# Order of the first products of each pass, of the sums of their weights, and of cf's column sums

## The chip, the cores and the metric

One NeuronCore of one Trainium2 chip runs the whole program, in float32. The metric is the device time of one execution in microseconds (us); the kernel before takes 1213.07 us (median of three runs, 1211.28 to 1214.89). Engines: TensorE (PE, with its weight loads PEld), VectorE (DVE), ScalarE (ACT), GpSimd (POOL) and SyncE (SP, whose queue issues most transfers).

## The reference

x holds 32 sequences of 64 tokens with 1024 features. The layer is an attention block and an expert ffn, each behind a linear map with a low-rank addition:

```python
x = x + attn(cond(x, label))       # cond: x W1' + rank 32, by the sequence's label
x = x + ffn(cond2(x, language))    # cond2: x W2' + 8 experts of rank 16, top 2 by logits
# attn: q, k, v = x Wqkv' + b; rotary q, k; 32 heads of 32, 8 of k and v; causal softmax; Wo
# ffn:  x W3' + b + 8 experts of rank 16, top 2 by softmax
```

## The kernel before

**Folded weights.** A first stage, *gen*, multiplies consecutive linear maps together, so that the tokens pass each composed matrix once. Its multiplications are *cq* and *ckv* (W1 with Wqkv: 1024 × 1024 and 1024 × 512) and *cf* (W2 with W3, 1024 × 1024; the residual's identity is added on its diagonal). The composed matrices go to scratch memory in DRAM (cqkv, and cf7, which already holds the sums that the ffn's products need).

**Products.** Every large multiplication is a `Group` (line 231), which computes a 2 × 2 block product with seven block products instead of eight. A block product (`mult`, line 259) is four calls of matmul over the chunks of the inner dimension. In the profile that is eight MATMUL instructions, 3.43 us for 512 columns. The left factors are blocks of the weights ("11", "12", "22") or their sums s1 to s4, which `weight_sums` (line 172) makes on GpSimd with four instructions, in the order s1, s3, s2, s4 of lines 179, 181, 180, 182. The right factors are blocks of the tokens or of the other matrix, or their column sums t1 to t4, which `column_sums` (line 185) makes on VectorE, four instructions each, on lines 191, 193, 195, 197. The products accumulate in three PSUM banks x, y and z:

| step | product | bank | what follows |
|---|---|---|---|
| p1 | 11 × 11 | x | ScalarE copies it to a sum p (line 282) |
| p6 | s2 × t2 | y | VectorE: u1 = y + p (line 288) |
| p5 | s1 × t1 | z | |
| p7 | s3 × t3 | y | VectorE: u2 = y + p (line 300) |
| p2 | 12 × 21 | x | output (0,0) |
| p4 | 22 × t4 | y | output (1,0) |
| p3 | s4 × 22 | z, after output (1,1) has left it | output (0,1) |

**Two passes.** After gen, the loop over `hf` (line 897) takes 1024 tokens a pass. A pass begins with the 16 instructions of the column sums of x (line 912), and then the query and key projections in five pairs of 128-row blocks, first pair 4 (the keys), then pairs 0 and 1. `qk_pair(g)` (line 950) loads the pair's weights from cqkv (SyncE's queue), has their sums made on GpSimd and gives a `RankGroup` (line 375). Its `main(begun, held)` runs the steps p1, p6, p5, p7, p2, then the rank rows and the outputs (`together`), p4 and p3, from step number `begun` on. The output of each pair is rotated on VectorE and GpSimd (`rope`, line 930). In the first pass the weights of pairs 4 and 0 are loaded ahead, during gen. In the second pass, low-rank matmuls (`ranks`, line 448) are woven between p1, p6 and the rest. Weight tiles have two buffers, and so have their sums. Pairs 2 and 3, the attention units, v and the output projection follow.

**The ffn** ends a pass: seven block products, each cut into two quarters, each quarter again a Group. In a `quarter` (line 1385) the function `known` adds on GpSimd what is already known of an output to the sum just made (line 1407); VectorE adds that to the PSUM bank on line 1425, which frees the bank for the next product.

**What sets the order.** A planner orders each engine's instructions by program order, by when it reckons their inputs ready, and by a cost table. Inside `manual_schedule` the named engines keep the program's order: SyncE, TensorE and VectorE in gen; TensorE and GpSimd in the ffn; all engines from pair 2 to the end of the output projection. The first pairs of a pass lie between, and there the planner decides, except for TensorE's first steps in the second pass. `tc.issue_after(ins)` makes what its block issues on the engine of `ins` stand behind `ins` in that engine's queue. It orders the queue alone; instructions on other engines, transfers among them, are untouched.

Of the kernel before, what the change touches and what calls it, by code (L numbers as in the profile page):

```python
# [13 lines left out]
F32 = mybir.dt.float32  # L14
# [5 lines left out]
P = 128  # L20
# [56 lines left out]
def block_kernel(ctx: ExitStack, tc: tile.TileContext, a, out: bass.AP):  # L77
    nc = tc.nc
# [16 lines left out]
    def tmp(name):  # L95
        return tp.tile([P, 512], F32, tag="t", name=name)
# [5 lines left out]
    late = {}  # L102
# [12 lines left out]
    def load_x(hf):  # L115
        t = [xp.tile([P, TH], F32, tag=f"x{kc}", name=f"x{kc}_{hf}") for kc in range(KC)]
        for kc in range(KC):
            nc.sync.dma_start(t[kc], a["xT"][kc, :, hf * TH : (hf + 1) * TH])
        return t
# [6 lines left out]
            engines={mybir.EngineType.SP, mybir.EngineType.PE, mybir.EngineType.DVE}  # L126
# [104 lines left out]
    class Group:  # L231
# [26 lines left out]

        def mult(self, ps, left, right, first=False):
            for kc in range(self.h):  # L260
                nc.tensor.matmul(  # L261
                    ps,
                    self.weights[left][:, kc, :],
                    self.right(right, kc),
                    start=first and kc == 0,
                    stop=kc == self.h - 1,
                    skip_group_check=True,
                )
# [154 lines left out]
    def load_w(from_, name):  # L423
        w = wp.tile([P, KC, WG], F32, tag="w", name=f"w_{name}")
        nc.sync.dma_start(w, from_)
        return w
# [74 lines left out]
    def differences(dst, src, n):  # L501

        v = src[:, : n * 2 * P].rearrange("p (g r o) -> p g r o", r=2, o=P)
        nc.gpsimd.tensor_sub(dst, v[:, :, 0, :], v[:, :, 1, :])

    with tc.tile_pool(name="gen", bufs=1) as gen:
# [43 lines left out]
        def sums_of(name, right, n):  # L550

            t = Columns(halves(right, n), n // 2, H, [None] * 4)

            def make(*which):
                for j in which:
                    s = gen.tile([P, H, 512], F32, tag=f"sum{j}", name=f"sum{j}_{name}")
                    t.tiles[j] = [s[:, kc, :] for kc in range(H)]
                    for kc in range(H):
                        t.make(kc, (j,))

            return t, make
# [67 lines left out]
        t_cf, make_cf = sums_of("cf", w3, D)  # L629
# [54 lines left out]
        def load_w3(w):  # L684
# [6 lines left out]
                (0, "p1"): lambda w: b1kv_rows[1](),  # L691
                (0, "p7"): lambda w: done_later(),
                (1, "p4"): load_w3,
                (3, "out11"): lambda w: make_cf(0, 1),
            },
        )
        make_cf(2, 3)
        differences(b1d, b1q, 5)
        b2 = hp.tile([P, TH], F32, tag="hw", name="b2").rearrange("p (k o) -> p k o", o=P)
        nc.sync.dma_start(b2, a["b2"])  # L700
# [190 lines left out]
    def scoped(name, bufs=1, side="left"):  # L891
        return pools.enter_context(tc.tile_pool(name=name, bufs=bufs, side=side, reuse_waits="tile"))
# [4 lines left out]
    for hf in range(2):  # L897
        x = first_pass["x"] if hf == 0 else load_x(hf)
# [23 lines left out]
        def low_half(c, low=low):  # L922
            return low.rearrange("p (b c t) -> p b c t", c=2, t=S)[:, :, c, :]
# [26 lines left out]
        def qk_pair(g, z_bank=group_bank):  # L950
            w = first_pass.pop(f"w{g}", None)
            if w is None:
                w = load_w(cqkv[:, :, g * WG : (g + 1) * WG], f"qk{hf}{g}")

            def out(r, c, ps, add):
                oc = 2 * g + r
                raw = tmp(f"raw_{hf}_{oc}_{c}")
                bias = bqk[:, oc : oc + 1]
                if add is None:
                    nc.scalar.activation(raw, ps, AF.Identity, bias=bias)  # L960
                else:
                    nc.vector.scalar_tensor_tensor(raw, ps, bias, add, ALU.add, ALU.add)
                rope(oc, c, raw)

            def rank(r, c, rows):
                b = b1d[rows, g, :] if (r, c) == (0, 1) else b1q[rows, (2 * g + r) * P : (2 * g + r + 1) * P]
                return b, low_half(c)[rows]

            return RankGroup(f"qk{hf}{g}", w, weight_sums(w, f"qk{hf}{g}"), xt, out, rank, z_bank)
# [119 lines left out]
                    av[b].rearrange("p (i m t) -> p i m t", i=2, t=S),  # L1089
                )  # L1090

        pair = qk_pair(4)
        if hf == 0:
            pair.p1()
        else:
            with tc.manual_schedule(engines={mybir.EngineType.PE}):
                for do in first_halves:
                    do()
                pair.p1()
                for do in second_halves + (pair.p6,) + sums:  # L1100
                    do()
        pair.main(1 + hf)
        for g in (0, 1):
            held, pair = pair, qk_pair(g, (ps_tile, group_bank)[g])
            pair.main(held=held)
        pair.last_rows()
        pair.out01()
        if hf == 0:
# [62 lines left out]
        with tc.manual_schedule():  # L1171

            rotated()
            pair, held = qk_pair(2), None
            for u in range(2):
# [14 lines left out]
                if u == 0:  # L1190
                    held, pair = g, qk_pair(3, ps_tile)
# [14 lines left out]
            for u in range(4):  # L1206
                first, second = 2 * u + 1, 2 * u + 2
# [62 lines left out]
            yp = scoped(f"sums_y{hf}", side="right")  # L1270
# [87 lines left out]
        w = wp.tile([P, KC, WG], F32, tag="w", name=f"w_h{hf}")  # L1358
# [20 lines left out]
        hw, acc, ring = {}, {}, []  # L1379

        def accumulator(x):
            pool, tag = {"a": (yp, "sum3"), "b": (fp, "b"), "z": (yp, "sum2"), "c": (None, None)}[x]
            acc[x] = acc["a"] if x == "c" else pool.tile([P, 4, 512], F32, tag=tag, name=f"{x}_f{hf}")

        def quarter(n, q):

            step, _, _ = SEVEN[n]

            if len(ring) < 2:
                ring.append(wp.tile([P, KC, WG], F32, tag="w", name=f"w_f{hf}{q}"))  # L1390
            w = ring[q].rearrange("p s (k o) -> p s k o", o=P)
            for part in (slice(0, 3), slice(4, 8)):
                nc.sync.dma_start(
                    w[:, part].rearrange("p s k o -> p (s k) o"),
                    cf7[:, n, part, :, q].rearrange("p s k o -> p (s k) o"),
                )
            prior, kept = acc.get(PRIOR.get(step)), acc.get(KEPT.get(step))
            r, c = OUT.get(step, (None, None))
            outs = {}

            def part(t, m, half):
                return t[:, 2 * q + m, half * 256 : (half + 1) * 256]

            def known(m, half, add):
                if prior is not None:
                    to = part(prior if kept is None else kept, m, half)
                    nc.gpsimd.tensor_add(to, part(prior, m, half), add)

            def out_f(m, half, ps, add):
                if prior is not None:  # L1410
                    add = part(prior if kept is None or add is None else kept, m, half)
                if kept is not None:
                    if add is None:
                        nc.scalar.copy(part(kept, m, half), ps)
                    else:
                        nc.vector.tensor_add(part(kept, m, half), ps, add)
                    return
                oc = 4 * r + q + 2 * m
                both = m in outs
                if not outs and q:  # L1420
                    outs["pair"] = fp.tile([P, 2, 512], F32, tag="gates", name=f"o_{hf}_{step}")
                if not both:
                    outs[m] = outs["pair"][:, m] if q else tmp(f"o_{hf}_{oc}_{c}")
                o = outs[m][:, half * 256 : (half + 1) * 256]
                nc.vector.scalar_tensor_tensor(o, ps, bb[:, oc : oc + 1], add, ALU.add, ALU.add)
                if both:
                    nc.scalar.dma_start(out[oc, :, hf, c, :], outs[m])

            def extra(m, half):
                differs = (m, half) == (0, 1)  # L1430
                for i, b in enumerate(experts_b):
                    if step == "p3":
                        lhs = bd[:, i, 8 + q if differs else q + 2 * m]
                    elif differs:
                        lhs = bd[:, i, 4 + 2 * r + q]
                    else:
                        oc = 4 * r + q + 2 * m
                        lhs = b[:, oc * P : (oc + 1) * P]
                    yield lhs, hw[i][c][:, half * 256 : (half + 1) * 256]

            group = Quarter(
                f"f{hf}{n}{q}",
                {name: w[:, i] for i, name in enumerate(FACTORS)},
                None, ts[n], out_f, extra if step in OUT else None, known, (group_bank, ps_tile)[q],
            )
            group.n_q = n, q
            return group
# [15 lines left out]
        with tc.manual_schedule(engines={mybir.EngineType.PE, mybir.EngineType.Pool}):  # L1463
# [17 lines left out]
            for n in range(7):  # L1481
                step = SEVEN[n][0]
                if step in KEPT:
                    accumulator(KEPT[step])
# [125 lines left out]
```

## Time and profile before

| | before |
|---|---|
| median of three runs | 1213.07 us |
| the profiled execution | 1214.05 us |
| its span, first to last instruction | 1212.3 us |
| PE busy | 1191.3 us (98%) |
| DVE busy | 701.6 us (58%) |
| POOL busy | 533.7 us (44%) |
| mean granted TensorE clock | 0.996 |
| TensorE's waits for other engines, in total | 16.3 us |

All times inside the profile count from the start of the span. Gen reaches to about 298 us, the first pass to about 752 us, the second to the end. A group of instructions is written as output <- inputs by the program's names: `qk_x`, `qk_y`, `qk_z` are the banks of a query and key pair, `f_x` to `f_z` those of the ffn, `cf_x` to `cf_z` those of cf; `s_qk` are sums of weights, `sum_x` and `sum_cf` column sums, `w_qk` weights. Buffer numbers are left out, so pairs 4 and 0 have the same names. A wait names the engine and line that ended it.

### The profile page before, as it was taken

How to read it: one execution, taken by the hardware profiler on the slowest of the kernel's cores; microseconds unless marked ns; L12 is line 12 of the kernel's file. 1: busy time of each engine (PE TensorE's matmuls, PEld its weight loads, DVE VectorE, ACT ScalarE, POOL GpSimd, SP SyncE). 2: the span in 40 equal slices, each digit the busy share in tenths (PEclk: the TensorE clock that was granted, in tenths of full speed). 3: DMA queues.
4: the chain of work that ended last, by engine and by line, in shares of the span. 5: the costliest groups of instructions: out<-in, count | busy, mean ns of one | idle time of the engine just before them, and what ended most of it. 6: DMA issues, size and time to landing. Idle time of an engine off the chain costs nothing.

```text
span 1212.3 us, 15157 instructions
## 1 busy us (share of the span) xinstructions
PE 1191.3 (98%) x5916; PEld 705.9 (58%) x5916; DVE 701.6 (58%) x1221; ACT 156.6 (13%) x302; POOL 533.7 (44%) x477
## 2 busy tenths in 40 slices
PE   9999999999899999999999998999999999999998
PEld 3444864554344458644458887444458644448887
DVE  4312162619356788774657552556788864657562
ACT  1000000000000114530011000100113530011000
POOL 3341364242244655761814533434655761812231
PEclk9999999999899999999999999999999999999999
DMA  6662744858111120222316665121120222304543
GB/s 243 220 210 102 267 143 144 293 164 285 48 63 35 35 71 1 71 70 70 103 31 193 194 193 159 48 66 35 35 70 2 71 70 70 102 24 112 157 140 103
DMA packets 114679, 136.71 MB, mean 113 GB/s; under 512 B 6576, under 2 KB 92976, under 8 KB 113328
## 3 DMA queue, kind: packets, MB, share of 16 engines
q1 hardware_dynamic: 101120, 111.52, 28.9%
q10 hardware_dynamic: 10800, 15.84, 3.7%
q0 software_dynamic: 2688, 8.39, 2.1%
q8 instruction: 47, 0.77, 0.3%
q14 instruction: 24, 0.20, 0.0%
HBM read 101.02 MB, written 34.71 MB: 112 GB/s over the span
## 4 chain that ended last, share of the span: by engine, by line
PE 92%; DVE 4%; DMA 2%; issue 1%; POOL 0%; SPq 0%; DVEq 0%; POOLq 0%
PE qk_y L261 9%; PE o_y L261 7%; PE f_y L261 6%; PE qk_z L261 6%; PE qk_x L261 6%; PE v L990 5%; PE o_x L261 5%; PE o_z L261 5%; PE f_z L261 4%; PE f_x L261 4%; PE cq_y L261 3%; PE cf_y L261 3%; PE sc L1011 3%; PE pt L1064 2%; PE cq_z L261 2%; PE f_z L273 2%
## 5 line engine op out<-in xcount | busy, mean ns | idle before, releaser
L938 POOL TENSOR_TENSOR raw<-raw,consts 128x512 f32<-128x512 f32 x40 | 63.1, 1587 | 112.8 <-DVE t L937 112.8
L1044 POOL TENSOR_TENSOR e<-e,top 128x512 f32<-128x512 f32 x64 | 64.9, 1044 | 57.3 <-DVE top L1043 42.2
L261 PE MATMUL f_y<-s_f,w_f 128*128 128x256 f32 x336 | 82.2, 380 | 0.5 <-DVE f_u L300 0.5
L1056 POOL TENSOR_TENSOR e<-e,tot 128x512 f32<-128x512 f32 x64 | 66.2, 1066 | 27.2 <-DVE tot L1054 27.2
L261 PE MATMUL qk_x<-x,w_qk 128*128 128x512 f32 x160 | 74.3, 606 | 0.0
L261 PE MATMUL qk_y<-sum_x,s_qk 128*128 128x512 f32 x160 | 72.3, 595 | 0.0
L261 PEld LDWEIGHTS f_y<-s_f,w_f 128*128 128x128 f32 x336 | 63.7, 190 | 9.6 <-DVE f_u L300 0.9
L261 PE MATMUL o_x<-q,w_o 128*128 128x512 f32 x128 | 58.9, 592 | 0.0
L990 PE MATMUL v<-w_v,x 128*128 128x256 f32 x256 | 58.7, 382 | 0.0
L1165 POOL TENSOR_TENSOR x<-x,o_u 128x512 f32<-128x512 f32 x24 | 30.9, 1292 | 54.5 <-DVE o_u L1163 33.2
L261 PEld LDWEIGHTS qk_x<-x,w_qk 128*128 128x128 f32 x160 | 30.7, 194 | 39.6 <-issue 39.5
L261 PEld LDWEIGHTS qk_y<-sum_x,s_qk 128*128 128x128 f32 x160 | 30.4, 191 | 37.6 <-issue 37.1
L990 PEld LDWEIGHTS v<-w_v,x 128*128 128x128 f32 x256 | 47.4, 190 | 8.4 <-issue 2.7
L939 DVE TENSOR_TENSOR t<-t,consts 128x512 f32<-128x512 f32 x40 | 48.7, 1228 | 0.7
L1053 DVE TENSOR_REDUCE tot<-e 128x8 f32<-128x512 f32 x64 | 40.5, 667 | 10.6 <-ACT e L1048 10.4
L1048 ACT ACTIVATE e<-e 128x512 f32<-128x512 f32 x64 | 38.2, 639 | 54.3 <-POOL e L1044 54.2
L1034 DVE TENSOR_TENSOR e<-sc,consts 128x512 f32<-128x512 f32 x64 | 39.7, 676 | 8.8 <-PE sc L1011 8.8
L261 PE MATMUL qk_z<-sum_x,s_qk 128*128 128x512 f32 x80 | 37.4, 608 | 6.8 <-POOL s_qk L179 6.8
L948 DVE TENSOR_TENSOR q<-raw,t 128x512 f32<-128x512 f32 x32 | 38.4, 1205 | 2.5 <-POOL raw L938 2.3
L1043 DVE TENSOR_REDUCE top<-e 128x8 f32<-128x512 f32 x64 | 39.6, 674 | 0.0
L261 PEld LDWEIGHTS o_x<-q,w_o 128*128 128x128 f32 x128 | 23.7, 190 | 26.8 <-issue 26.8
L179 POOL TENSOR_TENSOR s_qk<-w_qk 128x512 f32<-128x512 f32 x10 | 19.8, 1976 | 42.9 <-DMA w_qk<-cqkv 42.9
(364 smaller groups left out, 2399.5 us busy)
## 6 DMA issues: line engine op xcount, KB each, us to landing
w_f<-cf SPq DMA_DIRECT2D x28, 512.0 KB, 4.2
w_f<-cf SPq DMA_DIRECT2D x28, 384.0 KB, 7.4
w_qk<-cqkv SPq DMA_DIRECT2D x10, 1024.0 KB, 8.7
x<-in_xT SPq DMA_DIRECT2D x16, 512.0 KB, 7.6
w_o<-in_wo SPq DMA_DIRECT2D x16, 512.0 KB
s_o<-wos SPq DMA_DIRECT2D x16, 512.0 KB, 6.1
outT<-o ACTq DMA_DIRECT2D x20, 256.0 KB, 3.9
cqkv<-cq ACTq DMA_DIRECT2D x16, 256.0 KB, 2.5
```

Of the source, the lines that this page charges most:

```text
L261: nc.tensor.matmul(ps, self.weights[left][:, kc, :], self.right(right, kc), start=first and kc == 0, stop=kc == self.h - 1, skip_group_che ...
L938: nc.gpsimd.tensor_mul(rv, rv, c3)
L939: nc.vector.tensor_mul(t2v, t2v, s3)
L948: nc.vector.tensor_add(*unfinished.pop())
L990: nc.tensor.matmul(begun[t], x[kc][:, t * P : (t + 1) * P], wv[:, kc, :], start=False, stop=kc == KC - 1, skip_group_check=True,)
L1011: nc.tensor.matmul(sc[j][:, n * S : (n + 1) * S], q[rows, g, b, 2 * mp : 2 * mp + 2, :].rearrange("p m t -> p (m t)"), k[rows, g, b, :], s ...
L1034: nc.vector.tensor_add(per_key(e), per_key(sc[j]), mask.unsqueeze(1).to_broadcast([P, 8, S]))
L1043: nc.vector.tensor_reduce(top, ev, AX.X, ALU.max)
L1044: nc.gpsimd.tensor_sub(ev, ev, wide(top))
L1048: nc.scalar.activation(e, e, AF.Exp, scale=SCALE)
L1053: nc.vector.tensor_reduce(tot[:, i], es[i], AX.X, ALU.add)
L1056: nc.gpsimd.tensor_mul(es[i], es[i], wide(tot[:, i]))
```

## The change

Four edits, none of which changes what is computed:

- `mult` remembers its last matmul.
- cf's column sums: t1 alone is made after step out11 of ckv's last group, and t2 joins t3 and t4 after ckv's last step.
- In the first pass, pair 4's p1, p6, p5 and p7 run on TensorE in that written order. In both passes, TensorE's instructions of pairs 0 and 1 stand behind the last matmul of p7 (first pass) or p6 (second pass) of pair 4.
- In the second pass, GpSimd's instructions of `qk_pair(4)`, the four sums of its weights, stand behind the last `known` sum of the first pass's ffn. (The rewritten `accumulator` does what it did.)

```diff
@@ mult
-                nc.tensor.matmul(
+                self.last = nc.tensor.matmul(
@@ ckv
-                (3, "out11"): lambda w: make_cf(0, 1),
+                (3, "out11"): lambda w: make_cf(0),
             },
         )
-        make_cf(2, 3)
+        make_cf(1, 2, 3)
@@ the first pairs of a pass
-        pair = qk_pair(4)
+        with tc.issue_after(late["sum"].ins) if hf == 1 else ExitStack():
+            pair = qk_pair(4)
         if hf == 0:
-            pair.p1()
+            with tc.manual_schedule(engines={mybir.EngineType.PE}):
+                for do in (pair.p1, pair.p6, pair.p5, pair.p7):
+                    do()
         else:
...
-        pair.main(1 + hf)
+        first = pair.last
+        pair.main((4, 2)[hf])
         for g in (0, 1):
             held, pair = pair, qk_pair(g, (ps_tile, group_bank)[g])
-            pair.main(held=held)
+            with tc.issue_after(first.ins):
+                pair.main(held=held)
@@ known, in the ffn
-                    nc.gpsimd.tensor_add(to, part(prior, m, half), add)
+                    late["sum"] = nc.gpsimd.tensor_add(to, part(prior, m, half), add)
```

## Prediction

> **What bounds the kernel now.** I read the page first (shares of busy time), then who waited for whom on TensorE, then the chain that ended last, then the timeline around each wait.
>
> ```profile
> PE 1191.3 (98%) x5916; PEld 705.9 (58%) x5916; DVE 701.6 (58%) x1221; ACT 156.6 (13%) x302; POOL 533.7 (44%) x477
> ```
>
> TensorE's waits for other engines (total us, count, longest):
>
> ```profile
> PE qk_z L261 <- POOL s_qk L179: 6.8, 1, 6.8
> PE f_z L261 <- DVE o_p L1425: 4.0, 1, 4.0
> PE cf_x L261 <- ACT cf_p L282: 1.6, 1, 1.6
> ...
> PE cf_y L261 <- DVE cf_u L300: 0.8, 1, 0.8
> ```
>
> TensorE sets the end, so only its own waits and its slow stretches can be won. The three largest waits lie exactly where the change works: one in the first pass, one between the passes, one at the start of cf. I call them A, B and C.
>
> A. The timelines of TensorE, then Pool, at the start of the first pass (start, length):
>
> ```profile
> 298.38 3.60 PE L261 MATMUL qk_x<-x,w_qk 128*128 128x512 f32 x8
> 308.76 2.08 PE L261 MATMUL qk_z<-sum_x,s_qk 128*128 128x512 f32 x2 [6.79 <-POOL s_qk L179]
> 310.63 3.62 PE L261 MATMUL qk_x<-x,w_qk 128*128 128x512 f32 x4
> 314.05 3.67 PE L261 MATMUL qk_y<-sum_x,s_qk 128*128 128x512 f32 x8
> ```
>
> ```profile
> 278.88 1.34 POOL L182 TENSOR_TENSOR s_qk<-w_qk,s_qk 128x512 f32<-128x512 f32 x1
> 307.45 1.26 POOL L179 TENSOR_TENSOR s_qk<-w_qk 128x512 f32<-128x512 f32 x1 [27.23 <-DMA w_qk<-cqkv]
> ```
>
> Pair 4's four sums of weights end at 280.22. The sums at 307.45 belong to pair 0, whose weights had just landed. So the qk_z at 308.76 is one chunk (two of the eight instructions) of pair 0's p5, which the planner put between pair 4's p1 and p6; everything of pair 4 stands behind it. Counting confirms it: by the rank rows at 326.23 there are 10 qk_z instructions, and pair 4's p5 has 8. TensorE is idle 6.79, and then slow:
>
> ```profile
> 302.00:309.00 7.00, 0.23 (x1) 0.24 (x2) 3.43 (x6) 0.59 (x1) 1.55 (x2) 0.88 0.68 214
> 309.00:314.50 5.50, 5.50 (x7) 2.21 (x8) 0.00 (x0) 0.00 (x0) 3.41 (x3) 0.53 0.10 6
> ```
>
> The columns are length, busy time and count of PE, PEld, DVE, ACT and POOL, then the granted clock: 0.53 after the idle stretch.
>
> B. The chain at the seam of the passes (start, length, what):
>
> ```profile
> 743.05 6.59 DMA w_qk<-cqkv
> ...
> 752.26 1.22 POOL s_qk L180
> 753.48 0.69 POOL a_f L1407
> 754.17 0.03 issue
> 754.19 0.49 DVE o_p L1425
> 754.69 0.04 issue
> 754.73 2.08 PE f_z L261 x4
> ```
>
> Pool waits for the next pass's weights until 749.64 and makes three of their sums. The ffn's last sum a_f (L1407) stands behind them, though its input f_u was made at 748.24 to 748.66. VectorE's output needs a_f, and the last product f_z needs the bank which that output frees.
>
> C. TensorE waits 1.60 at 175.63 for the copy cf_p. ScalarE gives that copy only after it has issued the stores of ckv, which VectorE made at 173.54, behind eight column sums of cf.
>
> [...] at A two instructions take 2.08 and four take 3.41, where eight take 3.43 warm; B's 4.02 idle slows f_z too. [...] a_f is ready 4.8 us and doesn't pass. [...] one Pool sum at 762.98 took 6.58 instead of 1.26 during the x column sums, and VectorE's cf sums took up to 1.79 instead of 0.68 beside Pool's.
>
> **The change part by part.** None of it adds an instruction, a transfer or a semaphore that something must reach; it moves order.
>
> *First pass.* After p1 (ends 301.9) the order is p6, p5, p7, then the rest; pair 0 stands behind p7. p6 needs Pool's s2 of pair 4 (280.22 at latest) and the column sum t2, made at 298.12 to 300.61: ready. p5 from 305.3 needs t1 (298.2). p7 from 308.8 needs t3 (303.0) and VectorE's read of bank y after p6; VectorE is busy with t4 to 305.43 and reads in 0.69, so 306.1: ready. p7 ends at 301.9 + 3 × 3.43 = 312.2. Pair 0's sums end at 308.71, 309.93, 311.15 and 312.49, so even if pair 0's p5 comes at once, its operand s1 is 3.5 us old. Won: 6.79 idle, and 2.08 + 3.41 − 6 × 0.429 = 2.91 of slow clock: 9.70. What covers the late weights is the 10.3 us of p6, p5 and p7; without it the wait returns. Next late is pair 1's load, which needs pair 4's weight buffer. It moves with pair 4's end, has 8.7 (landing, median row of w_qk) plus 5.0 (four Pool sums) = 13.7 to do, under pair 0's eight products, 27.5. No cost. Bounds: 0 (wait comes back) to 9.7; I take 9.7.
>
> The same hold in the second pass stands behind p6; nothing of pair 0 runs before that now, as p1, p6, p5, p7 run from 759.87 to 777.7 without a wait. Value 0.
>
> *Second pass's sums.* a_f runs on an idle Pool as soon as f_u is there: 748.75 to 749.5 (a quarter before, the same sum starts 0.09 after f_u). VectorE's o_p ends near 750.0, f_y's last matmuls end at 750.6, f_z follows at once. Won: 4.02, and 2.08 + 1.48 − 1.73 (the same eight instructions at 742.00 to 743.72) = 1.83 of slow clock: 5.85. Now the cover. f_z ends near 752.3, so everything after comes 5.9 earlier: rank matmuls to 753.9, p1 to 757.5 (its weights landed at 749.64), rank matmuls to 759.7, then p6. p6 needs s2 and t2. Only the fourth Pool sum moves, ahead by 0.7: the first three keep 749.77 to 753.47. The x column sums follow VectorE's last output, now at about 752.8. They meet Pool's last two sums: [...] VectorE begins at 754.7 and t2 is there 8 × 0.61 = 4.9 later, at 759.6[...]. p6 wants it at 759.7. So 0, at worst some 0.3. Queued behind pair 4's sums on Pool are pair 0's: their weights land some 5 earlier (they wait for f_z's buffer), they may be shut out until VectorE is through at 762.5 to 764.5, and finish by 769.6; pair 0's p6, the first to need them, is near 792.7 − 5.9 = 786.8. The load itself on SyncE's queue isn't moved. Bounds: −0.3 (all of it comes back[...]) to 5.85; I take 5.85.
>
> *cf's column sums.* VectorE now does t1 (four), the two ckv outputs (2 × 0.41), then t2, t3, t4. ckv's banks are full at 167 and 168.7, so no new wait. The ckv outputs come at about 170.1 to 170.9 instead of 173.54; cf_p follows before 174, and p2 needs no wait: 1.60 won. But p7 (186.26) starts when VectorE's cf_u ends (186.22), behind t4, and VectorE is busy from 164.4 to 185.3 with the same work. p6, now at 177.5, needs t2, there by about 174. What remains is that the outputs[...] can run while Pool's L182 (to 171.26) shuts out t2's first sum: some 0.6 of 0.74. [...] all of 1.60 and the 0.23 before p7; if t3 and t4 fall worse, −1. I take 0.6.
>
> **Sum** against the profiled execution: 9.70 + 5.85 + 0.60 = 16.15. Span 1212.30 − 16.15 = 1196.15; 1.75 lies around it (1214.05 − 1212.30): 1197.90. The median of the runs is 0.98 below that execution: 1196.9, which I call 1197.0. Behind each place no wait of TensorE over 1 us is left and all loads hang on released buffers, so the gains run through to the end.
>
> **Rivals.**
> 1. [...] The x column sums, 5.9 earlier, shut out Pool's s2, as they did a sum at 762.98: s2 at 763.9, p6 waits 4.2 plus 1.8 slow, all of B: 1202.9. For: that 6.58. Against: Pool is first there by 3 us.
> 2. *A's wait moves.* With pair 0 held, planner or tile slots put another wait into p6 to p7, or behind p7 at pair 0: 9.7 lost, 1206.7. For: temporaries are being stored until about 304. Against: u1 wants its slot only at 305.4, and the second pass runs this order clean.
> 3. *The other side: pair 1's weights become late.* Its load waits for pair 4's last product p3. If the planner, given new edges, sets p3 so late that only one product of pair 0 is left (3.43), TensorE is idle 13.7 − 3.43 = 10.3 plus 2.9 slow, in each pass: 26.4, so 1223.4. It decides from 5.2 idle a pass (2 × (5.2 + 2.9) = 16.2), that is with fewer than 8.5 us, or 2.5 products, left. For: that region's order is the planner's, which has already misjudged a load once. Against: pair 4 comes first in the program, and now p3 runs at 330.83 and 785.82, before all but two instructions of pair 0.
> 4. *It doesn't do what it says*: the planner finds another order with the same waits: 1213.
>
> **How the numbers follow.** Forecast 0.72, rivals 0.07, 0.09, 0.08, 0.04 in order. Within 0.3% (3.6 us, also the spread of the three runs) is about what can't be told from no change. Faster: 0.72 + 0.07 + 0.09 = 0.88; same 0.04; slower 0.08. The forecast alone, with C's bounds and a run's spread, is 1194 to 1200; the range reaches over rivals 1 and 2, to 1207.5, and leaves out 3 and 4, 0.12.
>
> **What would show it.** A: four unbroken products after qk_x, no qk_z wait on s_qk, clock 1.0. B: L1407 ahead of L179 on Pool, no wait of f_z on o_p, x column sums near 753. C: ckv's outputs near 170.5, no wait of cf_x on cf_p, and p7 still right behind cf_u. The forecast is wrong if pair 0 or pair 1 waits for s_qk in either pass, or if p6 near 759.7 waits for sum_x or s_qk.

## The result and the profile after

The changed kernel takes 1199.43 us (median of four runs, 1199.19 to 1203.33) against 1212.64 us (median of four) for the kernel before on the same chip: a ratio of 0.9897, 95% interval 0.9871 to 0.9922, 1.0% faster. The forecast was 1197.0. The profiled execution took 1199.29, its span is 1197.5, which is 14.8 us less than before.

TensorE's waits (total us, count, longest) after the change:

```profile
PE h L458 <- issue: 1.8, 1, 1.8
...
PE qk_x L261 <- ACT qk_p L282: 0.7, 1, 0.7
```

The three waits A, B and C of the prediction (6.8, 4.0 and 1.6) are gone. New are 1.8 us inside the rank matmuls h, which no engine released, 0.7 us of qk_x for ScalarE's copy, and 0.4 us at the start of gen, where cq_x waits for its weights.

A, TensorE's timeline at the start of the first pass, now:

```profile
296.38 3.60 PE L261 MATMUL qk_x<-x,w_qk 128*128 128x512 f32 x8
300.65 2.84 PE L261 MATMUL qk_x<-x,w_qk 128*128 128x512 f32 x6 [0.68 <-ACT qk_p L282]
303.33 3.60 PE L261 MATMUL qk_y<-sum_x,s_qk 128*128 128x512 f32 x8
306.76 3.60 PE L261 MATMUL qk_z<-sum_x,s_qk 128*128 128x512 f32 x8
310.20 3.60 PE L261 MATMUL qk_y<-sum_x,s_qk 128*128 128x512 f32 x8
```

No chunk of pair 0 is there, but the order is not p1, p6, p5, p7, p2: six of p2's eight instructions stand right behind p1. They write bank x again, so they wait 0.68 us for the copy that takes p1 out of it. The stretch from p1's start to the rank rows is 18.20 us (296.38 to 314.58) instead of 27.85 (298.38 to 326.23); pair 0's two instructions, 0.86, now come later, so the gain is 9.65 − 0.86 = 8.8.

B, GpSimd's and then TensorE's timeline at the seam:

```profile
737.94 0.72 POOL L1417 TENSOR_TENSOR a_f<-a_f,f_u 128x256 f32<-128x256 f32 x1 [6.99 <-DVE f_u L300]
739.08 1.27 POOL L179 TENSOR_TENSOR s_qk<-w_qk 128x512 f32<-128x512 f32 x1 [0.42 <-PE f_y L261]
```

```profile
739.75 1.03 PE L261 MATMUL f_z<-sum_y,w_f 128*128 128x256 f32 x4
...
743.15 3.70 PE L261 MATMUL qk_x<-x,w_qk 128*128 128x512 f32 x8
746.78 1.21 PE L458 MATMUL h<-x,q 128*32 128x64 f32 x71
749.79 1.02 PE L458 MATMUL h<-x,q 128*32 128x64 f32 x57 [1.80 <-issue]
750.74 3.70 PE L261 MATMUL qk_y<-sum_x,s_qk 128*128 128x512 f32 x8
```

a_f runs first, f_z follows f_y without a wait, and its four instructions take 1.03 us instead of 2.08. From the last f_y instructions to p1 it was 9.68 us (750.12 to 759.80) and is 3.83 (739.32 to 743.15): 5.85 won. Then 1.80 is given back in the middle of the 128 rank matmuls behind p1.

C: p7 of cf's first group starts 15.59 us after its p1 (184.37 − 168.78), before 17.68 (186.26 − 168.58): 2.1 won here, and 2.0 at the first pass's start. p7 no longer stands right behind VectorE's cf_u, as the prediction had it: cf_u ends at 181.83, and p7 follows p5. In all 2.0 + 8.8 + 5.85 − 1.80 = 14.85, the whole of the 14.8.

### The profile page after: what moved, and what is told of

Same layout as the page of the kernel before. It is cut to its first block, busy times and chain, and to the rows that moved or that the text cites. A ratio compares the mean times of both kernels' runs of the same rounds, so it can differ in the third digit from the quotient of the medians.

```text
span 1197.5 us, 15158 instructions
## 1 busy us (share of the span) xinstructions
PE 1186.4 (99%) x5916; PEld 703.9 (59%) x5916; DVE 695.5 (58%) x1221; ACT 156.9 (13%) x302; POOL 533.5 (45%) x477
## 4 chain that ended last, share of the span: by engine, by line
PE 98%; DMA 1%; SPq 0%; issue 0%; DVE 0%; ACT 0%
PE qk_y L261 9%; PE o_y L261 7%; PE f_y L261 6%; PE qk_x L261 6%; PE qk_z L261 6%; PE v L990 5%; PE o_x L261 5%; PE o_z L261 5%; PE f_x L261 4%; PE f_z L261 4%; PE cf_y L261 3%; PE cq_y L261 3%; PE sc L1011 3%; PE pt L1064 2%; PE cq_z L261 2%; PE f_z L273 2%
## 5 line engine op out<-in xcount | busy, mean ns | idle before, releaser
L1066 ACT COPY ws<-pt 128x512 f32<-128x512 f32 x64 | 33.0, 612 | 41.8 <-PE pt L1064 41.8
L261 PE MATMUL qk_y<-sum_x,w_qk 128*128 128x512 f32 x80 | 37.0, 605 | 0.0
```

Source lines behind the costliest of these rows:

```text
L261: self.last = nc.tensor.matmul(ps, self.weights[left][:, kc, :], self.right(right, kc), start=first and kc == 0, stop=kc == self.h - 1, sk ...
```

## The experiments

**Which edit of the first pass carries its gain.** The written order without the hold:

```diff
-            with tc.issue_after(first.ins):
-                pair.main(held=held)
+            pair.main(held=held)
```

> The changed kernel without the hold (pairs 0 and 1 free again), the written order of p1, p6, p5, p7 kept. Theory 1, the hold carries the first pass's gain, since an order written among pair 4's own products does not keep pair 0's chunk of p5 out: the wait of qk_z on s_qk is back at 5 to 7.5 us with some 3 us of slow clock, and the gain of 8.8 us at that place is gone: about 1208 us. Theory 2, the written order carries it, as the prediction's step has it: no such wait, 1199 us.

1207.12 us, ratio 0.9950 (0.9933 to 0.9966). TensorE's waits in its profile, which is of the slowest of its four executions, 1209.39:

```profile
PE qk_z L261 <- POOL s_qk L179: 6.2, 1, 6.2
PE h L458 <- issue: 2.3, 1, 2.3
```

Theory 1 holds: from p1's start to the rank rows it is 27.15 us (296.30 to 323.45), nearly what it was before the change. The built program says why: here are TensorE's instructions from the last of p1 on, without the hold and as changed (sums of weights 1548 are pair 0's, 1480 pair 4's).

```
without the hold                             as changed
qk_x<-x_0_204,w_qk_1256                      qk_x<-x_0_204,w_qk_1256
qk_z<-sum_x_1458,s_qk_1548                   qk_x<-x_0_205,w_qk_1256
qk_x<-x_0_205,w_qk_1256                      qk_x<-x_0_206,w_qk_1256
qk_x<-x_0_206,w_qk_1256                      qk_x<-x_0_207,w_qk_1256
qk_y<-sum_x_1459,s_qk_1480 x4                qk_y<-sum_x_1459,s_qk_1480 x4
```

The written order binds the four products to each other. It does not keep anything else from coming between. Built with the hold and without the written order, the program has every engine's instructions in the same order as the changed kernel, from end to end, so it was not timed: the hold alone carries the gain, and the written order adds nothing.

**What the seam is worth, and whether the new wait belongs to it.** GpSimd's sums of weights free again:

```diff
-        with tc.issue_after(late["sum"].ins) if hf == 1 else ExitStack():
-            pair = qk_pair(4)
+        pair = qk_pair(4)
```

> The changed kernel with the second pass's sums of weights free again. If the seam's gain is the 5.85 us of the prediction, of which 1.8 us come back as the later wait of TensorE inside the rank matmuls: f_z waits for o_p again (about 4 us, and slow clock after), the wait of 1.8 us is gone, the time is 4.0 us above the changed kernel, 1203.5 us. If the 1.8 us have nothing to do with the seam they stay, and the time is 5.85 us above it, 1205.3 us.

1204.26 us, ratio 0.9928 (0.9911 to 0.9944), 4.8 above the changed kernel (the kernels before of the two comparisons differ by 0.5). f_z waits for o_p again, and the wait inside h is gone:

```profile
PE f_z L261 <- DVE o_p L1434: 4.5, 1, 4.5
```

In the profile 4.6 us of the difference lie at the seam (from f_y's last two instructions to p6, 740.46 to 756.44, against 739.32 to 750.74) and 1.0 at cf, of which below. From f_y's last two to p1 it is 10.25 us here and 3.83 in the changed kernel. So the held sums are worth 6.4 at f_z, against free sums in the same kernel, and 1.9 of that turn into the later wait.

**What cf's move is worth.** First the move alone on the kernel before, then the changed kernel without it (the diff of the change, forwards and backwards).

> The kernel before with the move of cf's column sums alone. Theory 1, the gain of 2 us at cf came with the move, because t3 now begins before GpSimd's second four sums of weights[...]: 1.6 to 2.1 us less than before (1210.6 us), t3 and t4 take 2.5 us each, and one GpSimd sum of s_cf is drawn out to over 3 us. Theory 2, it came from weights that happened to land 2.8 us earlier in that profile: GpSimd begins its first sums near 165 again, t1 takes over 5 us, t3 is slow, and the gain is 0 to 0.7 us.

> The changed kernel with cf's column sums in their old places. Theory 1, the move's own worth is the 1 us that it shows alone, and the rest of the 2 us in the changed kernel's profile came from cf's first weights landing 3 us earlier there: 1 us above the changed kernel, 1200.4 us, and if these weights land near 162 us in this profile, p7 of cf's first group starts near 184.4 us as in the changed kernel. Theory 2, the move is worth 2 us: 1201.4 us, with p7 near 186 us wherever the weights land.

Alone: 1212.03 us, ratio 0.9992 (0.9983 to 1.0001). Without it: 1200.08 us, ratio 0.9891 (0.9876 to 0.9905), 0.65 above the changed kernel. Neither median is clear of the noise: the first interval reaches 1, and the runs of the second (1199.65 to 1200.30) overlap those of the changed kernel. The profiles show some 1 us, not 2: p7 comes 16.55 us after p1 with the move alone and 17.68 before, 16.48 without the move and 15.59 in the changed kernel. The first run lies between its two theories: GpSimd's first sums began late, at 165.47, and still 1.1 us were won in its profile. Its timeline of VectorE:

```profile
173.57 4.62 DVE L195 TENSOR_TENSOR sum_cf<-w 128x512 f32<-128x512 f32 x4
178.12 5.68 DVE L197 TENSOR_TENSOR sum_cf<-w,sum_cf 128x512 f32<-128x512 f32 x4
```

and that of the changed kernel, VectorE and GpSimd:

```profile
172.23 2.48 DVE L195 TENSOR_TENSOR sum_cf<-w 128x512 f32<-128x512 f32 x4
174.64 2.48 DVE L197 TENSOR_TENSOR sum_cf<-w,sum_cf 128x512 f32<-128x512 f32 x4
```

```profile
162.19 1.27 POOL L179 TENSOR_TENSOR s_cf<-w_cf 128x512 f32<-128x512 f32 x1 [3.20 <-DMA w_cf<-in_w]
...
174.82 3.42 POOL L179 TENSOR_TENSOR s_cf<-w_cf 128x512 f32<-128x512 f32 x1 [6.74 <-DMA w_cf<-in_w]
```

In the changed kernel cf's first weights land early: GpSimd is through with their four sums at 168.09 and begins the next at 174.82, so t2 and t3 run beside an idle GpSimd, 2.48 each. Only t4 meets the next sums; it keeps its 2.48, and GpSimd's sum is drawn out to 3.42. With the move alone the first four sums last until 171.89, t2 is drawn out to 3.96, and t3 and t4 alternate with the next sums (1.57 to 1.71 each) and take 4.62 and 5.68. Leaving out the runs with thirty padding matmuls, nine profiles have the move. In seven, the changed kernel's among them, the weights landed so that GpSimd began at 162.15 to 163.01, and p7 came 15.58 to 15.59 us after p1; in the other two it began at 165.05 (the run with free sums above) and 165.47, and p7 came 16.55 us after p1. The load is issued at 156.7 to 157.5 each time. In the early runs its last packet came by 162.6. In the late ones, and in the kernel before, the last seven or eight of its 144 packets came one at a time, some 0.35 us apart, until 164.4 to 165.0. Why they do, and whether the old order profits as much from an early landing, stays open; without the move there are only 164.98 (17.68) and 163.79 (16.48).

**What the wait in h is.** It stands after 71 of 128 instructions, at no border of the program. Padding at the start of the kernel, small matmuls on zeros, shifts the instruction stream (each makes two pairs of weight load and matmul: with thirty the trace counts 66 matmuls there instead of 6):

```diff
-    for n in (512, 512, 128):
+    for n in (512, 512, 128) + (64,) * 10:      # and * 30
```

> The changed kernel with 10 more small matmuls on zeros in the warm-up at the start (20 instruction pairs on TensorE, in time that it waits for the first weights). The wait of 1.8 us in the rank matmuls of the second pass stands after 71 of 128 instructions. Theory 1, it is the fetch of the next block of TensorE's instructions, late because the 1 MB load of pair 0's weights goes first: the block's end moves 20 pairs ahead, so the wait stands after 51, begins some 0.3 us earlier, and lasts 1.8 to 2.3 us; the time stays at 1199.4 us. Theory 2, an operand of the 72nd instruction arrives late: the wait stays after 71.

> The same with 30 small matmuls (60 pairs). Theory 1: the block's end now stands after 11 of the 128[...]: no wait, and 1.8 us less, 1197.6 us. Theory 2: the wait stays after 71, 1199.4 us.

With ten, 1199.34 us, ratio 0.9885 (0.9870 to 0.9899), and TensorE's timeline shows the border moved by the 20 pairs:

```profile
747.38 0.97 PE L458 MATMUL h<-x,q 128*32 128x64 f32 x51
750.05 1.31 PE L458 MATMUL h<-x,q 128*32 128x64 f32 x77 [1.71 <-issue]
```

With thirty the wait is gone, as expected. From f_z to p6 it is 8.96 us (743.12 to 752.08) against 10.99 in the changed kernel (739.75 to 750.74). The time did not follow: 1202.19 us, ratio 0.9910 (0.9897 to 0.9923). The padding itself held the first product back from 5.47 to 11.56, and 3.4 us of that were left at cf (p1 at 172.17 instead of 168.78). Pair 4's p7 in the second pass also waited 0.6 for VectorE, which is new. So the wait in h is TensorE's next instructions, not an operand: its place moved from 71 to 51 with the 20 pairs. What delays them is tested by moving the one large transfer of those microseconds (shortened):

```diff
-                w = load_w(cqkv[:, :, g * WG : (g + 1) * WG], f"qk{hf}{g}")
+                w = wp.tile([P, KC, WG], F32, tag="w", name=f"w_qk{hf}{g}")
+                load = nc.sync.dma_start(w, cqkv[:, :, g * WG : (g + 1) * WG])
+                if (hf, g) == (1, 0):
+                    tc.add_manual_dep(load.ins, late["p1"].ins.name, Sync)
...
                 pair.p1()
+                late["p1"] = pair.last               # pair 4's last matmul of p1
```

> The changed kernel, with the load of pair 0's weights in the second pass made to wait for pair 4's p1 (it starts near 747 instead of 741 us, lands near 753.5; its sums are needed near 772). Theory 1, the block of instructions is late because it is fetched behind this 1 MB load: it now comes before it, the wait of 1.8 us in the rank matmuls is gone or under 0.3 us, and the time falls by 1.4 to 2 us, to about 1197.6 us. Rival, the fetch is late by itself (it is asked for late): the wait stays, 1199.4 us.

1197.79 us (1197.31 to 1198.79), ratio 0.9873 (0.9856 to 0.9889); the changed kernel in the same comparison 1199.34 (1198.62 to 1199.91). The transfers of the instruction queue (packets, MB, share), in the changed kernel from 747 to 748 and with the late load from 743 to 744; in each, the microseconds from 741 up to that one hold none:

```profile
q8 instruction: 1, 0.02, 6.7%
```

```profile
q8 instruction: 1, 0.02, 8.9%
```

TensorE's timeline with the late load:

```profile
743.34 3.70 PE L261 MATMUL qk_x<-x,w_qk 128*128 128x512 f32 x8
746.97 1.99 PE L458 MATMUL h<-x,q 128*32 128x64 f32 x128
748.90 3.70 PE L261 MATMUL qk_y<-sum_x,s_qk 128*128 128x512 f32 x8
```

The instructions come 4 us earlier, and all 128 run through. The theory holds: the block of instructions came at 747.35 behind the 1 MB of pair 0's weights and comes at 743.2 ahead of it. A store of 256 KB, which had stood behind that load too, comes earlier with it (0.25 MB from 743 to 744; in the changed kernel 0.20 from 746 to 747).

Before the change the same transfer also came behind this load, at 762.3, but 2.3 us ahead of the border at 764.64. The trace shows no wait there; the 128 instructions took 2.21 us, with the late load 1.99. TensorE's timeline before the change:

```profile
763.43 2.21 PE L458 MATMUL h<-x,q 128*32 128x64 f32 x128
```

In the changed kernel it came at 747.35, 0.64 ahead of the border at 747.99, and TensorE went on 2.4 us after it. Two things make up the 1.65 us between them. The border comes 7.2 us after the load is issued (740.80) instead of 7.8 (756.84): behind the old stall four f_z instructions took 1.69 (756.60) at a granted clock of 0.63 (755 to 759), where they now take 1.03 (740.61) at 1.00; and the transfer came 6.55 us after the issue instead of 5.5, for which the runs give no reason.

**The order inside the first pass.** Three versions: p2 in the written order; p2 and pair 4's rank rows, with the padding; the same with cheaper padding (32 weight columns). `main` then begins at step 5 or 6.

```diff
-                for do in (pair.p1, pair.p6, pair.p5, pair.p7):
+                for do in (pair.p1, pair.p6, pair.p5, pair.p7, pair.p2):                  # first
+                for do in (pair.p1, pair.p6, pair.p5, pair.p7, pair.p2, pair.together):   # second, third
```

> The changed kernel with p2 added behind p7 in the written order of the first pass (and left out of the later steps). If the 0.68 us wait of qk_x for the copy qk_p comes only from six of p2's instructions standing right behind p1: it goes, p6 starts right behind p1 (its column sums are there), and the time falls by 0.7 to 1.0 us, to about 1198.5 us. If p6 then waits for its column sums or p7 for bank y: unchanged or slower by up to 1 us.

> shift30 with p2 and pair 4's rank rows behind p7 in the written order of the first pass, so that the three row groups stay together. If writing p2 alone won nothing because it left one rank row instruction to run by itself (1.05 us for z, where three together take 1.05 to 1.1), this keeps the 0.7 us of the wait for qk_p: no wait in the first pass, 0.7 us under shift30, 1196.9 us. If not: as shift30, 1197.6 us.

> The rows kernel with 30 matmuls on zeros of 32 weight columns as padding, which take less time at the start than the 30 of 128 columns, which held the first product back by 6 us and cost 3.3 us of the end: the padding should cost 0 to 1 us, the wait in the rank matmuls is gone, about 1197.5 us. If the padding holds the start back further, 1199 us or more.

The first: 1198.98 us, ratio 0.9885 (0.9868 to 0.9901), not told apart from the changed kernel. The wait of 0.68 went, but the planner moved z's rank row ahead, alone:

```profile
306.59 1.12 PE L385 MATMUL qk_z<-low,b1q 32*128 32x512 f32 x2
```

Left together, the three row groups start within 0.02 us of each other and all take 1.07 (314.58 to 315.65 in the changed kernel). So p1 to the end of the rank rows took 19.56 us (296.20 to 315.76) against 19.27. The second and third keep the rows together: 1202.17 us (six runs, one at 1208.75; ratio 0.9917, 0.9896 to 0.9937) and 1198.58 us (0.9876, 0.9859 to 0.9892). In the second the padding hides the gain again (p1 of cf at 173.50); in the third it costs 1.2 us there (169.93).

**A faster version.** The late load and the rows together, beside the changed kernel once more:

> late_load with p2 and the rank rows behind p7 in the written order of the first pass. From the profile of the run that had both the rows and the padding: another 0.7 to 1.0 us less, 1196.8 us. No wait of TensorE over 1 us is left but the one at the start.

> The changed kernel once more, for comparison on this chip: 1199.4 us, within 0.6 us.

1196.25 us (1196.08 to 1196.49), ratio 0.9858 (0.9841 to 0.9874), and 1199.34 us, ratio 0.9882 (0.9866 to 0.9899): 3.1 us under the changed kernel, with no overlap of the runs. In its profile p1 to the end of the rank rows is 18.32 us (296.30 to 314.62), 0.95 less, and TensorE waits for nothing over 1 us but the first memset (1.5).

## Why the prediction was right, and where it was not

The time lies in the range and the direction and mechanism of A and B are as forecast; the sum was 16.15 and the profiles differ by 14.8. That they lie so near is in part luck: A gave 0.9 less than forecast and B 1.8 less, and C's profile 1.4 more made up for half of it.

- *A, the order.* "After p1 (ends 301.9) the order is p6, p5, p7, then the rest" failed: six instructions of p2 came first, and their wait of 0.68 (with 0.2 that no wait accounts for) makes 8.8 of the 9.70. Giving the written order and the hold one common credit was a gap: the run without the hold lost the gain, and the hold needs no written order beside it. The slow clock, counted as 2.91, is gone: the granted clock is 1.00 from 296 to 316.
- *B.* 5.85 at f_z, as forecast. p6's operands: t2 was there at 748.65 and s2 at 742.82, so rival 1 did not come about, though a sum of pair 0, begun at 748.05, was drawn out to 6.54 again and ended 1.1 after VectorE's t4. t1 took 4.17 instead of 2.49 beside GpSimd's last sums (1.29 and 1.59).
- *B, what is late next.* "... all loads hang on released buffers, so the gains run through to the end" failed. The load did start earlier, with f_z's buffer; but TensorE's next instructions came behind it (before the change too, but 2.3 us ahead of their border instead of 0.64), and I had not looked for a transfer that is no operand. 1.8 us came back. That is the largest error of mechanism.
- *C.* Taken at 0.6, an estimate of mine, worth about 1 by the profiles with and without it. ckv's outputs did run beside a sum of GpSimd, 0.41 each (with the move alone, 169.02 to 169.76, beside the 1.72 from 168.51). The 2.0 of the profile holds another 1 us that goes with the early landing of cf's weights: luck, not the move. "VectorE is busy from 164.4 to 185.3 with the same work" failed there, as t4 ended at 177.12. The upper bound, 1.60 + 0.23 = 1.83, was reached.
- *From profile to median.* I took off 0.98 because the execution profiled before lay that much above its median. The one after lies 0.14 below its own. That, and not the change, is 1.1 of the 2.4 us between 1197.0 and 1199.43; the steps above are the other 1.3.

Rivals 2, 3 and 4 did not occur: there is no wait for s_qk in either pass, and pair 1 is not late.

## What to carry to other kernels

A written order among some instructions doesn't keep others out from between them; to keep one out, hold it behind a named instruction, and read the built order to see that it worked. When a stall is removed, list everything that moves in those microseconds, the transfers of instructions too: where a burst of short instructions follows a few microseconds after a large load, its next instructions can come too late behind that load (here a wait of 1.80 us, 7.2 us after a load of 1 MB was issued). Before moving a step past others, see what it ran beside: a row group that ran free beside two others can cost its full time alone (here the three took 1.07 together, and one took 1.12 alone).

## What was not expected of the hardware

- The page counts 47 transfers of instructions on one queue, 0.77 MB, some 16 KB each. That TensorE waited for one of them in the middle of a burst of short matmuls is shown by the border, which moved with the padding, 20 pairs for 20, and by the transfer, which came at 747.35 behind a 1 MB load and at 743.2 ahead of it. In three profiles with the wait TensorE went on 2.4 to 2.5 us after the transfer (747.35 to 749.79 in the changed kernel, 747.65 to 750.05 with ten padding matmuls, 755.85 to 758.34 without the hold; the transfers are placed to 0.1 us).
- A wait of 2.34 us was followed by the slow clock, as the 4.02 before the change was (0.54 from 754.7 to 758.2). The 2.34 is the wait in h in the run without the hold: the 57 matmuls behind it took 1.67 us instead of 1.02, and the granted clock was 0.55 from 758.3 to 760. After waits of 1.80 and 1.91 us (the changed kernel, twice) the same 57 took 1.02. What decides between the two is not shown.
- In these profiles VectorE and GpSimd on sums of 128x512 either alternate, or one shuts the other out for several instructions. In the changed kernel VectorE's t4, begun 0.18 us before a sum of GpSimd, took 2.48 and that sum 3.42, to 1.12 after t4's end. With the move alone t3, begun 0.84 us before such a sum, took 4.62 and the sum 1.57; before the change t3, begun 0.17 us after one, took 6.67 and the sum 1.26. So it is not only who is first; what else decides stays open.
